# A transformer block on one core: order of a batch's attention pieces, cross-attention's query and key weights as one matrix per head, and both input norms from one variance

## The chip, the core and the metric

The kernel runs on one core of a Trainium2 chip. The core has a matrix engine (TensorE; PE in the profile, and PEld for its loads of the stationary operand), three engines for elementwise work (VectorE = DVE, ScalarE = ACT, GpSimd = POOL) and a queue that only issues transfers (SyncE = SP). Each engine works through its own list of instructions in order and waits on semaphores for the others. TensorE writes its results to PSUM, from which DVE or ACT copy them to SBUF. The metric is the device time of one execution in microseconds. The kernel before took 962.75 us, the median of three runs (961.74 to 963.99).

## The reference

The input x has 16 batches of 128 tokens of 128 features, all in float32. It goes through four residual parts; each part sees the layer norm of the stream. The change touches only the first part, which has a self-attention, a cross-attention with 77 context tokens per batch and a gated feed-forward part. Cut to what matters:

```python
def layernorm(x, eps=1e-05):
    m = jnp.mean(x, axis=-1, keepdims=True)
    v = jnp.var(x, axis=-1, keepdims=True)
    return (x - m) * jax.lax.rsqrt(v + eps)

def adaln(x, t, w, b):
    scale, shift = jnp.split(t @ w + b, 2, axis=-1)
    return layernorm(x) * (1.0 + scale) + shift

def mha(xq, ctx, wq, wk, wv, wo, bo):        # H = 16 heads of DH = 64
    q, k, v = heads(xq @ wq), heads(ctx @ wk), heads(ctx @ wv)
    scores = jnp.einsum('bhqd,bhkd->bhqk', q, k) / math.sqrt(DH)
    attn = jax.nn.softmax(scores, axis=-1)
    out = jnp.einsum('bhqk,bhkd->bhqd', attn, v)
    return out.transpose(0, 2, 1, 3).reshape(b, sq, INNER) @ wo + bo

# first part, called with layernorm(x) as x
h1 = adaln(x, t, norm1_w, norm1_b)
x = mha(h1, h1, attn1_wq, attn1_wk, attn1_wv, attn1_wo, attn1_bo) + x
h2 = adaln(x, t, norm2_w, norm2_b)
x = mha(h2, context, attn2_wq, attn2_wk, attn2_wv, attn2_wo, attn2_bo) + x
h3 = adaln(x, t, norm3_w, norm3_b)
x = glu_ff(h3, ff_w1, ff_b1, ff_w2, ff_b2) + x
```

So the input is normed twice in a row: the part is given layernorm(x), and its own adaln norms that again. The other three parts (a mixture of experts with two of seven, an attention of slots over the context, and a mixture with one of eight) are as they were.

## The kernel before

The residual stream r and the input x0 stay in SBUF, tokens on the partitions. The attention works in groups of two batches: groups 0 to 7 are the self-attention (ph = 0), 8 to 15 the cross-attention (ph = 1). One batch of a group is a unit, and a unit's 16 heads are handled in two halves of eight (hg = 0, 1).

- `attn_prologue` (L235) prepares a group. In self-attention it norms the input into r (`ln_stats`, L173, then `normalize`, L200), norms r once more into z, and adds the output bias to r (`row_add`, L227, on POOL). `ln_stats` takes the bn_stats of each half of the features, seven small DVE instructions, and the power -1/2 on POOL (L170). TensorE transposes z (`ta`, L224), and ACT scales and shifts it into hT (L251). Then come the queries and the keys (`pq`, L267): 8 matmuls of 256 columns for the queries and 8 of 256 (self) or 154 (cross: 2 x 77 tokens) for the keys, copied by ACT two at a time (L268), and the values (`pv`, L272, copied at L276).
- `scores` (L279) takes one half of a unit: eight matmuls (`s`, L286) with 64 rows each, in which an even and an odd head lie on the two halves of the array's rows; then the softmax: maximum and subtraction on DVE (L294, L296), exponential on ACT (L297), sum and reciprocal on DVE (L299, L300), and the multiplication with the reciprocal on POOL (L301).
- `attend_t` (L304) transposes the weights of a half in two tiles of four heads (`te`, L311); ACT copies the first tile, DVE the second (L312).
- `attend_v` (L315) multiplies with the values (`po`, L321); ACT copies the first half's result, DVE the second's (L325).
- `attn_project` (L327) makes the output projection of a unit (`ya`, L331), and DVE adds it to r (L335).

PSUM has two buffers for the scores, two for the transposes and two for all else (projections of a group, `po` and `ya` in turn). The main loop (L379) is one unit ahead with the scores and one unit behind with the projection:

```python
            if i == 0:
                if g + 1 < NG:
                    states[g + 1] = attn_prologue(g + 1, ap_)
            ...
                e_next = [scores(states[g1], i1, hg, ap_) for hg in range(2)]
            oT = ap_.tile([P, 8, P], F32, name=f"oT{g}_{i}", tag="oT")
            eT = [attend_t(states[g], i, hg, e[hg], ap_) for hg in range(2)]
            if late:
                attn_project(*late)
            for hg in range(2):
                attend_v(states[g], i, hg, eT[hg], oT)
```

This text gives priorities and not the final order: a scheduler in the language's tile framework lays each engine's instructions into one list before the run, and takes later work into gaps that it foresees. The list is fixed from then on. In it the norms of all eight self-attention groups stand early on DVE, ahead of and between the first scores.

All weights are loaded at the start on SP's queue: attention's four blocks of 1 MB (`wa`, L108, two of them first and two at 13.9 us), the rest behind. The host lays them out in `_layout`; for each attention there is a block with wq and wk side by side and one with wv and wo.

## Time and profile before

| what | value |
|---|---|
| median of three runs | 962.75 us |
| the profiled execution | 961.27 us |
| its span, first to last instruction | 959.5 us |
| mean granted TensorE clock | 0.939 |
| busy share PE, DVE, ACT, POOL | 87%, 67%, 43%, 39% |
| attention, last addition to r | 488.5 us |
| one group of self-attention | 30.8 us |
| one group of cross-attention | 27.4 us |

The page's first part gives each engine's busy time in the span, its second part the busy share in 40 equal slices as one digit each. In the lists of groups a line gives the source line, the engine, the operation, what it writes and reads with the shapes, how many, busy time and mean duration, and the idle time of the engine ahead of it with what ended it. A line of the timeline gives start, duration, engine, source line, operation and count, and in brackets the idle time before it and what ended that. A line of the windows gives the stretch, its length, and for each engine the busy time with its number of instructions. A float32 matmul stands in the trace as two instructions; its end is modelled, so starts are safer to read than durations.

### The profile page before, as it was taken

The numbers are of one execution on the slowest core, as the hardware profiler recorded it, in microseconds if no ns is written. First come the engines' busy times: TensorE is split into PE (matmuls) and PEld (weight loads), VectorE is DVE, ScalarE is ACT, GpSimd is POOL, SyncE is SP. The second block draws the span as 40 slices with busy tenths as digits, with TensorE's granted clock in tenths as the row PEclk, the third lists the DMA queues.
The fourth block names the chain that finished last, engine by engine and source line by source line (L and its number), as shares of the span: only waits on it lengthen the run. The fifth ranks groups of instructions, "written<-read, shape, count | busy, mean of one in ns | idle before, by whom it ended". The sixth has DMA issues, their size and how long they took to land.

```text
span 959.5 us, 16967 instructions
## 1 busy us (share of the span) xinstructions
PE 830.1 (87%) x6155; PEld 660.3 (69%) x6155; DVE 646.5 (67%) x1946; ACT 416.5 (43%) x873; POOL 369.9 (39%) x416
## 2 busy tenths in 40 slices
PE   5799999999999999999999978999746677775597
PEld 4477767677687777777866647999645556654586
DVE  4896668766775654555867794555687776768454
ACT  2445554455444444554342211444135767552132
POOL 2442323222322211233252206776254544443476
PEclk9899999999999999999999988999859998976699
DMA  8100000000000000000020015998300000012794
GB/s 325 40 2 1 1 1 2 1 1 1 1 2 1 1 1 2 1 1 1 2 71 12 23 61 166 320 331 271 99 1 1 1 1 1 1 31 58 253 341 149
DMA packets 29422, 61.87 MB, mean 64 GB/s; under 512 B 4250, under 2 KB 17901, under 8 KB 28699
## 3 DMA queue, kind: packets, MB, share of 16 engines
q1 hardware_dynamic: 25067, 51.70, 15.9%
q0 software_dynamic: 4272, 9.09, 3.1%
q8 instruction: 49, 0.80, 0.3%
q14 instruction: 34, 0.28, 0.1%
HBM read 54.01 MB, written 7.23 MB: 64 GB/s over the span
## 4 chain that ended last, share of the span: by engine, by line
PE 56%; DVE 21%; POOL 8%; DMA 7%; ACT 4%; issue 4%; SPq 0%; POOLq 0%; ACTq 0%; DVEq 0%
PE pq L267 11%; PE s L286 6%; PE po L321 5%; PE pv L272 5%; PE te L311 5%; PE ya L331 4%; DMA res<-ysm,tom 3%; PE gum L735 2%; PE h1n L979 2%; ACT eT L312 2%; DMA zsm<-tok,frmm 2%; PE su L898 2%; DMA zsn<-tok,frmn 2%; PE ynn L994 1%; POOL ym L170 1%
## 5 line engine op out<-in xcount | busy, mean ns | idle before, releaser
L301 POOL TENSOR_TENSOR e<-e,ri 128x1024 f32<-128x1024 f32 (+1 forms) x64 | 99.9, 1562 | 297.5 <-DVE ri L300 129.1
L294 DVE TENSOR_REDUCE mx<-s 128x8 f32<-128x1024 f32 (+1 forms) x64 | 64.3, 1006 | 95.7 <-PE s L286 95.7
L267 PE MATMUL pq<-ha,wa 128*128 128x256 f32 x384 | 97.3, 406 | 0.9 <-ACT ha L251 0.9
L286 PEld LDWEIGHTS s<-k,q 64*128 64x128 f32 x1024 | 69.9, 187 | 40.6 <-issue 40.5
L286 PE MATMUL s<-k,q 64*128 64x128 f32 (+1 forms) x1024 | 87.0, 287 | 8.1 <-DVE e L296 8.1
L311 PE MATMUL te<-ident,e 128*128 128x128 f32 (+1 forms) x512 | 75.7, 280 | 12.9 <-ACT eT L312 12.0
L267 PEld LDWEIGHTS pq<-ha,wa 128*128 128x128 f32 x384 | 70.6, 198 | 19.0 <-ACT q L268 3.6
L299 DVE TENSOR_REDUCE ri<-e 128x8 f32<-128x1024 f32 (+1 forms) x64 | 64.0, 1001 | 21.0 <-ACT e L297 20.8
L331 PE MATMUL ya<-wa,oT 128*128 128x128 f32 x512 | 72.4, 275 | 0.0
L311 PEld LDWEIGHTS te<-ident,e 128*128 128x128 f32 (+1 forms) x512 | 55.6, 144 | 23.7 <-ACT eT L312 8.5
L312 ACT COPY eT<-te 128x512 f32<-128x512 f32 (+1 forms) x64 | 37.3, 582 | 79.6 <-PE te L311 79.5
L321 PE MATMUL po<-eT,v 128*64 128x128 f32 (+1 forms) x1024 | 69.9, 278 | 0.0
L297 ACT ACTIVATE e<-e 128x1024 f32<-128x1024 f32 (+1 forms) x64 | 56.9, 891 | 29.5 <-DVE e L296 28.6
L296 DVE TENSOR_TENSOR e<-s,mx 128x1024 f32<-128x1024 f32 (+1 forms) x64 | 64.3, 1007 | 3.9 <-DVE mx L294 0.5
L331 PEld LDWEIGHTS ya<-wa,oT 128*128 128x128 f32 x512 | 64.4, 192 | 0.4 <-ACT oT L325 0.4
L321 PEld LDWEIGHTS po<-eT,v 128*64 128x64 f32 (+1 forms) x1024 | 56.4, 136 | 7.2 <-ACT oT L325 0.8
L735 PE MATMUL gum<-zTnm,wm 128*128 128x128 f32 x456 | 61.3, 275 | 0.0
L735 PEld LDWEIGHTS gum<-zTnm,wm 128*128 128x128 f32 x456 | 56.8, 192 | 0.3 <-ACT zTnm L650 0.2
L268 ACT COPY q<-pq 128x512 f32<-128x512 f32 x64 | 37.3, 584 | 45.3 <-PE pq L267 45.3
L636 POOL DMA_INDIRECT zsm<-tok,frmm x38 | 36.9, 970 | 34.1 <-DVE secm L614 21.1
L276 ACT COPY v<-pv 128x512 f32<-128x512 f32 (+1 forms) x64 | 37.4, 584 | 21.8 <-PE pv L272 21.1
L312 DVE COPY eT<-te 128x512 f32<-128x512 f32 (+1 forms) x64 | 42.7, 669 | 5.3 <-PE te L311 5.3
(368 smaller groups left out, 1805.6 us busy)
## 6 DMA issues: line engine op xcount, KB each, us to landing
wm<-in_moe_w_dram SPq DMA_DIRECT2D x38, 576.0 KB, 5.1
wn<-in_moe_w_dram SPq DMA_DIRECT2D x23, 578.0 KB, 5.5
wa<-in_attn_w_dram SPq DMA_DIRECT2D x4, 1024.0 KB, 7.5
ygm<-res SPq DMA_DIRECT2D x8, 256.0 KB, 3.8
tok<-stm SPq DMA_DIRECT2D x4, 258.0 KB, 3.3
tok<-stn SPq DMA_DIRECT2D x4, 258.0 KB, 3.2
x<-in_x_dram SPq DMA_DIRECT2D x8, 128.0 KB, 7.1
cb<-in_rows_dram SPq DMA_DIRECT2D x1, 1024.0 KB, 8.7
```

The costliest lines, as they stand in the source:

```text
L267: PE.matmul(pq[:, j, :n], lhsT=wqk[:, w : w + P], rhs=src, start=True, stop=True)
L286: PE.matmul(ps[:, par, j * nk : (j + 1) * nk], lhsT=st["qT"][h0 : h0 + DH, c, i * P : (i + 1) * P], rhs=st["kT"][h0 : h0 + DH, c, i * nk : ...
L294: V.tensor_reduce(mx, pv, AX.X, ALU.max)
L296: V.tensor_tensor(e, pv, mx.unsqueeze(3).to_broadcast([P, 2, 4, nk]), ALU.subtract)
L297: S.activation(e, e, AF.Exp, scale=1.0 / math.sqrt(DH))
L299: V.tensor_reduce(ri, e, AX.X, ALU.add)
L301: G.tensor_tensor(e, e, ri.unsqueeze(3).to_broadcast([P, 2, 4, nk]), ALU.mult)
L311: PE.transpose(t[:nk, j, :], e[:, par, j, :], ident)
L312: (S.copy if par == 0 else V.tensor_copy)(eT[:nk, par], t[:nk])
L321: PE.matmul(po[par * DH : (par + 1) * DH, j, :], lhsT=st["v"][:nk, i, 8 * hg + 2 * j + par, :], rhs=eT[:nk, par, j, :], start=True, stop=True,
L331: PE.matmul(y, lhsT=oT[:, c, :], rhs=st["wo"][:, 1024 + c * D : 1024 + (c + 1) * D], start=(c == 0), stop=(c == 7),)
L735: PE.matmul(ps[j][:, c * P : (c + 1) * P], lhsT=w[:, k : k + P], rhs=zT, start=True, stop=True)
```

## The change

Three things are changed, and all of them lie in the attention.

- Order: in a unit the next unit's first half of scores, this unit's first half of transposes and the late projection now come ahead of the second half of scores and transposes; the products with the values follow at the end.
- Cross-attention's scores: for each head wq and wk are multiplied into one 128x128 matrix (`fold`, once, in place of wq and wk in SBUF, in the first two units of group 4; the host lays the two transposed for that). The keys become, for each head, that matrix times the context (16 matmuls of 154 columns, copied three at a time), the queries are hT itself, and the scores of four heads are one matmul with 128 rows and 4 x 77 columns.
- Norms: in self-attention both norms of the input come from one variance v. The first is (v + eps)^(-1/2); the norm of the normed input has the factor ((1 + eps) v + eps^2)^(-1/2) on x minus its mean. One power on POOL gives both, and z and r are both made from x0.

```diff
--- before.py
+++ after.py
@@ -197,6 +197,21 @@
         V.tensor_scalar(mean, mean, 0.5, None, ALU.mult)
         return rs, mean
 
+    def variance(src, p, n, nm):
+        st = sm.tile([P, 4, 6], F32, name=f"st{nm}", tag="st")[:p, :n, :]
+        for i in range(n):
+            V.bn_stats(st[:, i, :], src[:, i, :])
+        me, qe, mo, qo = (st[:, :, k] for k in (1, 2, 4, 5))
+        dm, mean, q = (small(nm, k, p, n, "") for k in ("dm", "mv", "qq"))
+        V.tensor_tensor(dm, me, mo, ALU.subtract)
+        V.tensor_tensor(q, qe, qo, ALU.add)
+        V.scalar_tensor_tensor(dm, dm, 0.25, dm, ALU.mult, ALU.mult)
+        V.scalar_tensor_tensor(q, q, 1.0 / D, dm, ALU.mult, ALU.add)
+        V.tensor_tensor(mean, me, mo, ALU.add)
+        V.tensor_scalar(mean, mean, 0.5, None, ALU.mult)
+        return q, mean
     def normalize(dst, src, rs, mean, n):
         for i in range(n):
             V.tensor_scalar(
@@ -232,18 +247,33 @@
     GB = 2
     GT = GB * P
 
-    def attn_prologue(g, ap_):
+    def attn_norm(g):
         ph, gi = divmod(g, B // GB)
         b0 = gi * GB
         rg = r[:, b0 : b0 + GB, :]
         z = zp.tile([P, 4, D], F32, name=f"za{g}", tag="z")
         if ph == 0:
             xg = x0[:, b0 : b0 + GB, :]
-            rs, mean = ln_stats(xg, P, GB, f"i{g}")
+            v, mean = variance(xg, P, GB, f"i{g}")
+            q = small(f"j{g}", "qj", P, 4, "")
+            V.tensor_scalar(q[:, GB:], v, 1.0 + LN_EPS, LN_EPS * LN_EPS, ALU.mult, ALU.add)
+            V.tensor_scalar(q[:, :GB], v, LN_EPS, None, ALU.add)
+            rs = rsqrt(q, P, 2 * GB, f"j{g}", "")
+            normalize(z, xg, rs[:, GB:], mean, GB)
             normalize(rg, xg, rs, mean, GB)
-        rs, mean = ln_stats(rg, P, GB, f"j{g}")
-        normalize(z, rg, rs, mean, GB)
+        else:
+            rs, mean = ln_stats(rg, P, GB, f"j{g}")
+            normalize(z, rg, rs, mean, GB)
         row_add(rg, R_BO1 if ph == 0 else R_BO2, GB)
+        return z
+    def attn_prologue(g, ap_):
+        ph, gi = divmod(g, B // GB)
+        b0 = gi * GB
+        rg = r[:, b0 : b0 + GB, :]
+        z = attn_norm(g)
         t = transpose_n(z, P, GB, f"a{g}")
         hT = zp.tile([P, 512], F32, name=f"ha{g}", tag="h")
         for i in range(GB):
@@ -256,16 +286,28 @@
         nk = P if ph == 0 else NC
         kvT = hT if ph == 0 else ctxT[:, b0 * NC : (b0 + GB) * NC]
         wqk, wvo = w_att[2 * ph], w_att[2 * ph + 1]
-        qT = ap_.tile([P, 8, GT], F32, name=f"q{g}", tag="q")
-        kT = ap_.tile([P, 8, GT], F32, name=f"k{g}", tag="k")
         v = ap_.tile([P, GB, H, DH], F32, name=f"v{g}", tag="v")
-        for dst, src, w0, n in ((qT, hT, 0, GT), (kT, kvT, 1024, GB * nk)):
-            for c in range(0, 8, 2):
-                pq = psM.tile([P, 2, 256], F32, name=f"pq{g}_{w0}_{c}", tag="mm")
-                for j in range(2):
-                    w = w0 + (c + j) * P
-                    PE.matmul(pq[:, j, :n], lhsT=wqk[:, w : w + P], rhs=src, start=True, stop=True)
-                S.copy(dst[:, c : c + 2, :n], pq[:, :, :n])
+        if ph == 0:
+            qT = ap_.tile([P, 8, GT], F32, name=f"q{g}", tag="q")
+            kT = ap_.tile([P, 8, GT], F32, name=f"k{g}", tag="k")
+            for dst, src, w0, n in ((qT, hT, 0, GT), (kT, kvT, 1024, GB * nk)):
+                for c in range(0, 8, 2):
+                    pq = psM.tile([P, 2, 256], F32, name=f"pq{g}_{w0}_{c}", tag="mm")
+                    for j in range(2):
+                        w = w0 + (c + j) * P
+                        PE.matmul(pq[:, j, :n], lhsT=wqk[:, w : w + P], rhs=src, start=True, stop=True)
+                    S.copy(dst[:, c : c + 2, :n], pq[:, :, :n])
+        else:
+            qT = hT
+            kT = ap_.tile([P, H, GB * NC], F32, name=f"k{g}", tag="k")
+            for c in range(0, H, 3):
+                m = min(3, H - c)
+                pq = psM.tile([P, 3, GB * NC], F32, name=f"pk{g}_{c}", tag="mm")
+                for j in range(m):
+                    w = (c + j) * D
+                    PE.matmul(pq[:, j, :], lhsT=wqk[:, w : w + D], rhs=kvT, start=True, stop=True)
+                S.copy(kT[:, c : c + m, :], pq[:, :m, :])
         for i in range(GB):
             for hh in range(2):
                 pv = psM.tile([P, 8, DH], F32, name=f"pv{g}_{i}_{hh}", tag="mm")
@@ -276,11 +318,38 @@
                 S.copy(v[:nk, i, hh * 8 : (hh + 1) * 8, :], pv[:nk])
         return dict(ph=ph, b0=b0, nk=nk, qT=qT, kT=kT, v=v, wo=wvo, g=g)
 
+    def fold(w, hg):
+        ps = psS.tile([P, 2, 512], F32, name=f"fold{hg}", tag="s")
+        wp = w[:, hg * 1024 : (hg + 1) * 1024]
+        for j in range(4):
+            for par in range(2):
+                h0 = par * DH
+                PE.matmul(
+                    ps[:, par, j * D : (j + 1) * D],
+                    lhsT=wp[h0 : h0 + DH, (4 + j) * D : (5 + j) * D], rhs=wp[h0 : h0 + DH, j * D : (j + 1) * D],
+                    start=True, stop=True,
+                )
+        for par, copy in enumerate((S.copy, V.tensor_copy)):
+            copy(wp[:, par * 512 : (par + 1) * 512], ps[:, par, :])
     def scores(st, i, hg, ap_):
 
         nk, nm = st["nk"], f"{st['g']}_{i}_{hg}"
         ps = psS.tile([P, 2, 512], F32, name=f"s{nm}", tag="s")
-        for j in range(4):
+        if st["ph"] == 1:
+            for par in range(2):
+                h0 = 8 * hg + 4 * par
+                PE.matmul(
+                    ps[:, par, : 4 * nk].rearrange("p (j k) -> p j k", k=nk),
+                    lhsT=st["qT"][:, i * P : (i + 1) * P],
+                    rhs=st["kT"][:, h0 : h0 + 4, i * nk : (i + 1) * nk],
+                    start=True, stop=True,
+                )
+        for j in range(4 if st["ph"] == 0 else 0):
             for par in range(2):
                 h0, c = par * DH, 4 * hg + j
                 PE.matmul(
@@ -377,21 +446,30 @@
         late = None
         glu_h = {}
         for n, (g, i) in enumerate(units):
+            if n in (8, 9):
+                fold(w_att[2], n - 8)
             if i == 0:
                 if g + 1 < NG:
                     states[g + 1] = attn_prologue(g + 1, ap_)
                 else:
                     glu_h[0] = glu_prologue(0)
             e = e_next
-            if n + 1 < len(units):
+            more = n + 1 < len(units)
+            if more:
                 g1, i1 = units[n + 1]
-                e_next = [scores(states[g1], i1, hg, ap_) for hg in range(2)]
+                e_next = [None, None]
             oT = ap_.tile([P, 8, P], F32, name=f"oT{g}_{i}", tag="oT")
-            eT = [attend_t(states[g], i, hg, e[hg], ap_) for hg in range(2)]
+            eT = [None, None]
+            if more:
+                e_next[0] = scores(states[g1], i1, 0, ap_)
+            eT[0] = attend_t(states[g], i, 0, e[0], ap_)
             if late:
                 attn_project(*late)
-            for hg in range(2):
-                attend_v(states[g], i, hg, eT[hg], oT)
+            if more:
+                e_next[1] = scores(states[g1], i1, 1, ap_)
+            eT[1] = attend_t(states[g], i, 1, e[1], ap_)
+            attend_v(states[g], i, 0, eT[0], oT)
+            attend_v(states[g], i, 1, eT[1], oT)
             late = (states[g], i, oT)
         attn_project(*late)
 
@@ -1081,7 +1159,11 @@
     )[None]
     attn = []
     for k in ("attn1_", "attn2_"):
-        attn.append(cat([a[l0 + k + "wq"], a[l0 + k + "wk"]], axis=1))
+        if k == "attn1_":
+            attn.append(cat([a[l0 + k + "wq"], a[l0 + k + "wk"]], axis=1))
+        else:
+            q, kk = (chunks(a[l0 + k + w].T) for w in ("wq", "wk"))
+            attn.append(cat([q[:, :512], kk[:, :512], q[:, 512:], kk[:, 512:]], axis=1))
         attn.append(cat([a[l0 + k + "wv"], chunks(a[l0 + k + "wo"])], axis=1))
     f = "L0_ffn_"
     gs = [a[f + "sg"], *a[f + "rg"]]
```

## The prediction

> **What bounds the kernel now.** I read the page's busy shares and slices first, then the two attention stages by windows, then the TensorE and VectorE timelines inside them.
>
> ```profile
> PE 830.1 (87%) x6155; PEld 660.3 (69%) x6155; DVE 646.5 (67%) x1946; ACT 416.5 (43%) x873; POOL 369.9 (39%) x416
> ...
> PE   5799999999999999999999978999746677775597
> ...
> PEclk9899999999999999999999988999859998976699
> ```
>
> The attention fills slices 1 to 21 (its last addition to r ends at 488.5 us). There PE is at 9 and the clock full. Two windows, one group of two batches each, tell self- from cross-attention:
>
> ```profile
> 188.60:219.50 30.90, 29.14 (x236) 22.13 (x234) 22.67 (x35) 15.12 (x26) 9.08 (x7) 1.00 0.00 1
> 333.90:361.30 27.40, 27.09 (x237) 21.30 (x236) 16.09 (x35) 13.23 (x24) 6.69 (x7) 1.00 0.01 1
> ```
>
> A self-attention group takes 30.8 us (the scale and shift of h at L251 comes every 30.8 us), a cross-attention group 27.4 with PE idle for 0.3. So in cross-attention PE's own work sets the time, and what is taken from it comes off the end. What that work is:
>
> ```profile
> L286 PE MATMUL s<-k,q 64*128 64x77 f32 x512 | 41.5, 281 | 0.0
> ...
> 334.88 3.80 PE L267 MATMUL pq<-ha,wa 128*128 128x256 f32 x16
> 338.52 0.77 PE L267 MATMUL pq<-ctxT,wa 128*128 128x154 f32 x4
> ...
> 352.95 2.01 PE L286 MATMUL s<-k,q 64*128 64x77 f32 x30
> ```
>
> Each f32 matmul is two passes in the trace. From start to start a pass of 512 columns takes 0.429 us, of 256 0.216, of 154 0.131, of 128 0.112. A score pass, 64 rows, two side by side, takes 0.062 (2.01/30, less its tail) for 77 columns and the same for 128.
>
> In self-attention PE also stands still, for its VectorE neighbours:
>
> ```profile
> 215.88 0.66 PE L311 MATMUL te<-ident,e 128*128 128x128 f32 x4 [1.44 <-ACT eT L312]
> ...
> 213.03 1.23 DVE L296 TENSOR_TENSOR e<-s,mx 128x1024 f32<-128x1024 f32 x1
> 214.18 1.22 DVE L294 TENSOR_REDUCE mx<-s 128x8 f32<-128x1024 f32 x1
> 215.31 0.68 DVE L312 COPY eT<-te 128x512 f32<-128x512 f32 x1
> ```
>
> The copy that frees a transpose buffer stands on DVE behind the subtraction and the maximum of the next scores. And at the start:
>
> ```profile
> 35.35 0.77 PE L286 MATMUL s<-k,q 64*128 64x128 f32 x2 [5.97 <-DVE e L296]
> ...
> 32.67 1.21 DVE L294 TENSOR_REDUCE mx<-s 128x8 f32<-128x1024 f32 x1
> ```
>
> the first scores are ready at 29.0, but DVE is in the norms until 32.7, and PE waits 6 us.
>
> **1. Cross-attention: one matrix per head (8 groups).** Counting each pass to the start of the next, the window 333.9 to 361.3 divides into: queries 3.64, keys 2.62, scores 4.93, projection 4.40, attention times values 3.95, transposes 3.74, values 3.72, ta 0.37; sum 27.4.
> Removed: the queries' 16 passes, 3.64. Keys become 16 matmuls, 32 passes x 0.131 = 4.19, and about 0.5 of waiting where an exponential (0.72) gets between ACT's copies: 4.7, that is +2.1. Scores become two matmuls of 308 columns with 128 rows per unit and half: 16 passes x 0.259 (0.216 at 256 columns, plus 52 at the slope up to 512) = 4.14, that is -0.8. The projection is no longer cut by transposes in the built order: 32 x 0.112 = 3.6, -0.8; the values' products are cut twice more by scores, +0.2. Sum -2.9; walking the built PE order with these durations gives 24.4, and I take **-3.0 a group**. Ends: -3.6 (only the durations at full rate) and -1.6 (projection as slow as now, keys at the 0.164 of today's passes).
> ACT has fewer copies (six of up to 462 columns for eight; 512 take 0.58, 308 take 0.42) and isn't the bound. Does the softmax keep up? From scores to normalized weights: 0.80 + 0.80 + 0.72 + 0.79 + 0.19 + 1.23 (L294, L296, L297, L299, L300, L301) and five hand-overs of 0.1: 5.0 us. In the built order the second half's transposes in a unit without prologue come 8.0 us after their scores, so 3 us are left. One group's prologue falls into self-attention's last window, so I count 7.8 groups: 7.8 x -3.0 = **-23.4** (-28.1 to -12.5).
>
> The row that decides the scores is the packed pass: 0.062 at 77 columns and at 128, so it pays for something that doesn't shrink with the moving columns; the 128 stationary ones of its load (PEld L286, 187 ns each, two at a time) are the nearest. The Trainium skill, page "TensorEngine Tiling (Array Packing)", section "Theoretical Speedup", speaks against this edit: contractions of up to 64 rows run up to twice as fast packed, which the new scores give up. Taken at its word, an estimate from that page, a group would gain some 1.1 instead of 3.0 and the sum would be -14; the row disagrees with it at 77 columns.
>
> **2. The order of a batch's pieces (self-attention).** Per unit it was scores 0, scores 1, transposes 0 and 1, projection, products; now scores 0, transposes 0, projection, scores 1, transposes 1, products. No instruction is added. In the built order DVE's chain from one second-half score is: subtraction until 3.0 us after these scores, exponential, sum until 5.3, maximum of the next scores until 6.4, reciprocal, then GpSimd 1.9: the last transposes start at 8.9, where PE was free at 8.2 (wait 0.7, in place of today's 1.44 and its like). Behind it DVE does subtraction, sum, maximum, subtraction, copy, z (held by GpSimd's multiplication, as the 1.48 us z at 219.03 is today) and sum again, and frees the buffer of the next group's second query pair only at 15.9, where PE is ready at 14.1 (wait 1.8). Then the projections run, one exponential costing 0.3, and the group closes at 30.05: **-0.75** a group. Ends: today's excess in the projection (6.02 us against 32 x 0.112) goes altogether, -2.4; or a copy falls behind one more subtraction and maximum (2 x 1.13), +2.3. Five steady groups: **-3.8** (-12 to +11.5).
>
> **3. One variance for both norms.** Eight powers of 4 columns (1.04, L170) replace sixteen of 2 (0.70), and half the statistics go. First group: the chain at 8.84 to 11.84 (r, statistics, power, z) becomes z alone, so its projections start at 10.9 instead of 13.3. But the second group's x lands at 13.9 as before, and DVE's queue then holds, per group, a power of 1.04 and a row addition of 0.73 on POOL in turn with 1.2 of r or z: about 3.2 with z, 2.6 without, instead of 4.8. The first maximum comes at 29.9, not 32.7, the subtraction that frees PE 2.7 us earlier; and the seventh and eighth group's statistics, which today hold the third maximum until 51.6 where its scores are done at 49.9, are gone by then: 2.7 + 1.6, less a little: **-4** (0, if the loads set it, to -6). Later in self-attention these steps lie early on DVE and cost PE nothing either way.
>
> **4. The fold.** 16 matmuls of 64 rows, 32 passes x 0.062 = 2.0, and four copies of 128x512 (0.58 ACT, 0.67 DVE) in the fifth group. Its weights were issued at 14.3 and landed within 9.1, long before. The copies lie beside projections; without that cover the two on DVE cost 1.3. It takes one of two score buffers, which were free by then: **+2.1** (0 if it falls into the waits of part 2, to +3.4). No DMA is added, SP's order is the same list, and behind the attention every engine's order is unchanged.
>
> Sum: -23.4 - 3.8 - 4 + 2.1 = -29.1. The profiled execution took 961.3 (span 959.5, 1.8 around it): 932.2. The median of the runs is 962.75, 1.5 higher, and so I predict **934**. Its own range is 922 to 946. A difference of 0.2%, 1.9 us, is about what a measurement can tell from none.
>
> **The rivals.**
> *The softmax takes PE's place in cross-attention.* If DVE's queue delays the second half's weights by over 3 us, the group stays at 27.4 and only parts 2 to 4 are left: -5.7, 957. For it: DVE's line of sum, maximum, subtraction, copy, z. Against it: DVE is busy 16.1 of 27.4.
> *Packing is worth a full half.* 77 columns at the slope of 0.429 for 512 are 0.065 a pass, two side by side 0.032. If that is what the 64 passes cost and the rest of their 4.93 is waiting that the new passes inherit, scores cost 1.1 more instead of 0.8 less, a group gains 1.1: -8.6 - 5.7, 948. For it: nothing but the arithmetic; against it 30 passes in 2.01 us without a stop. This is what the tiling page's rule would give here.
> *The new scores' operand is slow.* Their moving side is four stretches of 77, 154 apart; no row has that form. Between the 0.259 of the slope, which I take because all f32 rows follow it, and twice that (16 x 0.259 = 4.1 more): a group loses 1.2, +9.4 - 5.7, 966.
> *Slower: the second half's copy on DVE.* The products of the second half now follow their transposes at once, and the copy that they need (L312, DVE) stands behind the next scores' maximum and subtraction. Where PE has nothing to put between, it waits 2 x 1.13 in each of 16 units, and 2 x 0.71 in the 16 of cross-attention: +59, with the rest 993. It decides from half of that, about 0.9 us a unit. For it: PE waits 1.44 for just such a copy today. Against it: in the built order ta, scores and query projections stand before seven of the eight products.
> *It doesn't do what it says.* The scheduler could undo the order; but in the built order the scores, transposes and projection do stand as in the edit, so I give it nothing of its own.
>
> Chances: forecast 0.74; softmax 0.11, 957; packing 0.04, 948; slow operand 0.04, 966; copies 0.07, 993. Faster is 0.74 + 0.11 + 0.04, with little lost at the forecast's edges: 0.89; slower 0.10, same 0.01. The range leaves out the two slower cases and the far ends, where all bounds of parts 1 to 3 would fall together, and takes in the softmax case: 919 to 958.
>
> **What would show it.** Right: cross-attention's group 24 to 25 us, PE still above 95% there; score passes of 308 columns near 0.26 apart; L286's 64-row form gone from cross-attention; self-attention's group near 30; the first long wait of PE ending near 32.7; the attention's last addition to r near 460. Wrong: PE waits of over 1 us at transposes or products in cross-attention, self-attention's group over 31, or a fold that holds the scores.

## The result, and the profile after

The changed kernel takes 934.26 us (median of four runs, 931.10 to 938.01) where the kernel before takes 962.25 (961.70 to 963.99): a ratio of 0.971 with a 95% interval of 0.967 to 0.975. The profiled execution took 934.72 us, with a span of 933.0.

All of it lies in the attention. On VectorE's timeline the last addition to r of the kernel before and that of the changed kernel (start, duration, engine, line, operation, then the idle time before it and what ended that):

```profile
488.17 0.29 DVE L335 TENSOR_TENSOR r<-ya,r 128x128 f32<-128x128 f32 x1 [1.28 <-PE ya L331]
```

```profile
460.86 0.29 DVE L404 TENSOR_TENSOR r<-ya,r 128x128 f32<-128x128 f32 x1 [1.28 <-PE ya L400]
```

The attention ends 27.3 us earlier; behind it come 471.0 us before and 471.8 after (span less the end of that addition). The page of the changed kernel, busy share and slices:

```profile
PE 814.3 (87%) x5803; PEld 645.8 (69%) x5803; DVE 633.9 (68%) x1900; ACT 408.8 (44%) x859; POOL 366.9 (39%) x408
...
PE   6799999999999999999999969999557777684697
...
PEclk9899999999999999999999989999669898976799
```

352 TensorE instructions are gone, and the attention is still a row of nines, at full clock from the third slice on. One group of self- and one of cross-attention, in windows (stretch, length, busy time and instructions of PE, PEld, DVE, ACT, POOL, then granted clock and the share and rate of transfers):

```profile
183.30:212.80 29.50, 28.66 (x236) 22.23 (x236) 21.71 (x36) 15.06 (x24) 9.02 (x6) 1.00 0.01 2
344.50:369.10 24.60, 24.60 (x188) 19.05 (x188) 15.56 (x29) 11.90 (x23) 5.62 (x5) 1.00 0.00 1
```

In the window of cross-attention PE has no idle time at all. Below, the attention is cut where ACT starts to scale and shift h for groups 3, 8, 9 and 15 (groups counted from 0; 8 is the first of cross-attention), and at the last addition to r. Lengths in us, and the difference to the kernel before:

| kernel | start to group 3 | five groups of self-attention, 3 to 8 | the turn, 8 to 9 | six groups of cross-attention, 9 to 15 | group 15 to the end | attention's end |
|---|---|---|---|---|---|---|
| before | 96.1 | 154.2 | 28.9 | 164.2 | 45.1 | 488.5 |
| changed | 92.4 (-3.7) | 149.5 (-4.7) | 28.7 (-0.2) | 147.8 (-16.4) | 42.7 (-2.4) | 461.2 (-27.3) |

The experiments are read by the same cuts, because these tell smaller differences than whole runs: the time behind the attention goes from 464.8 to 474.3 us among kernels whose work there is the same, while the changed kernel, profiled twice on two chips, gave attention ends of 461.15 and 461.20.

### The profile page after: what moved, and what is told of

Its sections match the earlier page's. It is cut to its first block, busy times and chain, and to the rows that moved or that the text cites. A ratio compares the mean times of both kernels' runs of the same rounds, so it can differ in the third digit from the quotient of the medians.

```text
span 933.0 us, 16193 instructions
## 1 busy us (share of the span) xinstructions
PE 814.3 (87%) x5803; PEld 645.8 (69%) x5803; DVE 633.9 (68%) x1900; ACT 408.8 (44%) x859; POOL 366.9 (39%) x408
## 3 DMA queue, kind: packets, MB, share of 16 engines
q1 hardware_dynamic: 25067, 51.70, 16.4%
## 4 chain that ended last, share of the span: by engine, by line
PE 56%; DVE 24%; POOL 8%; DMA 5%; issue 3%; ACT 3%; SPq 1%; POOLq 0%; ACTq 0%; DVEq 0%
PE pv L314 6%; PE po L390 5%; PE pq L298 5%; PE gum L813 5%; PE ya L400 4%; PE te L380 4%; PE pk L309 4%; PE s L346 4%; DVE mx L363 3%; PE ynm L824 2%; DVE e L365 2%; PE h1n L1057 2%; DVE ri L368 2%; DMA zsn<-tok,frmn 2%; PE su L976 2%
## 5 line engine op out<-in xcount | busy, mean ns | idle before, releaser
L380 PE MATMUL te<-ident,e 128*128 128x128 f32 (+1 forms) x512 | 71.7, 276 | 4.8 <-POOL e L370 4.7
L390 PE MATMUL po<-eT,v 128*64 128x128 f32 (+1 forms) x1024 | 75.3, 279 | 0.5 <-DVE eT L381 0.3
L390 PEld LDWEIGHTS po<-eT,v 128*64 128x64 f32 (+1 forms) x1024 | 60.7, 137 | 15.5 <-DVE eT L381 8.6
L298 PE MATMUL pq<-ha,wa 128*128 128x256 f32 x256 | 66.4, 410 | 1.4 <-ACT ha L281 0.9
L400 PE MATMUL ya<-wa,oT 128*128 128x128 f32 x512 | 63.1, 276 | 0.0
L400 PEld LDWEIGHTS ya<-wa,oT 128*128 128x128 f32 x512 | 59.9, 192 | 1.1 <-ACT v L318 0.6
L298 PEld LDWEIGHTS pq<-ha,wa 128*128 128x128 f32 x256 | 47.7, 201 | 14.3 <-ACT q L299 2.4
L355 PE MATMUL s<-k,q 64*128 64x128 f32 x512 | 44.0, 290 | 7.4 <-DVE e L365 7.4
L355 PEld LDWEIGHTS s<-k,q 64*128 64x128 f32 x512 | 34.8, 188 | 17.8 <-issue 14.9
L735 POOL DMA_INDIRECT res<-ysm,tom x38 | 37.3, 982 | 16.4 <-ACT ysm L828 6.2
```

The costliest lines, as they stand in the source:

```text
L298: PE.matmul(pq[:, j, :n], lhsT=wqk[:, w : w + P], rhs=src, start=True, stop=True)
L355: PE.matmul(ps[:, par, j * nk : (j + 1) * nk], lhsT=st["qT"][h0 : h0 + DH, c, i * P : (i + 1) * P], rhs=st["kT"][h0 : h0 + DH, c, i * nk : ...
L380: PE.transpose(t[:nk, j, :], e[:, par, j, :], ident)
L390: PE.matmul(po[par * DH : (par + 1) * DH, j, :], lhsT=st["v"][:nk, i, 8 * hg + 2 * j + par, :], rhs=eT[:nk, par, j, :], start=True, stop=True,
L400: PE.matmul(y, lhsT=oT[:, c, :], rhs=st["wo"][:, 1024 + c * D : 1024 + (c + 1) * D], start=(c == 0), stop=(c == 7),)
```

## The experiments

**Each part alone, and the matrices without the shared load.** Four kernels on one chip, where the kernel before took 962.93 us (median of 29 runs). The first makes only the new order:

```diff
-                e_next = [scores(states[g1], i1, hg, ap_) for hg in range(2)]
...
-            eT = [attend_t(states[g], i, hg, e[hg], ap_) for hg in range(2)]
...
+                e_next[0] = scores(states[g1], i1, 0, ap_)
+            eT[0] = attend_t(states[g], i, 0, e[0], ap_)
             if late:
                 attn_project(*late)
-            for hg in range(2):
-                attend_v(states[g], i, hg, eT[hg], oT)
...
+                e_next[1] = scores(states[g1], i1, 1, ap_)
+            eT[1] = attend_t(states[g], i, 1, e[1], ap_)
+            attend_v(states[g], i, 0, eT[0], oT)
+            attend_v(states[g], i, 1, eT[1], oT)
```

> The kernel before with the new order of a unit's pieces alone. By the prediction's terms the order takes 3.8 us from self-attention and, in cross-attention, 0.8 a group from the projection that is no longer cut, less 0.2 for the products that are cut more often: 3.8 + 0.6 x 7.8 = 8.5, so 954. Rival 1, the matrix per head carries nearly all of the gain: 960 to 962. Rival 2, the order carries it and the matrix per head little: 940 to 945.

The second takes only cross-attention's matrices with the fold, in the old order and with two norms:

```diff
+            if n in (8, 9):
+                fold(w_att[2], n - 8)
...
-        for dst, src, w0, n in ((qT, hT, 0, GT), (kT, kvT, 1024, GB * nk)):
...
+        else:
+            qT = hT
+            kT = ap_.tile([P, H, GB * NC], F32, name=f"k{g}", tag="k")
...
```

> The kernel before with cross-attention's one matrix per head alone, in the old order. By the prediction's terms a group loses 3.64 of queries and 0.8 of scores and gains 2.1 of keys, 2.35 x 7.8 = 18.3, less 2.1 for the multiplication of the weights: 16, so 946. Rival 1: 936 to 938. Rival 2: 955 or more.

The third takes only the one variance:

```diff
-            rs, mean = ln_stats(xg, P, GB, f"i{g}")
+            v, mean = variance(xg, P, GB, f"i{g}")
...
+            rs = rsqrt(q, P, 2 * GB, f"j{g}", "")
+            normalize(z, xg, rs[:, GB:], mean, GB)
             normalize(rg, xg, rs, mean, GB)
-        rs, mean = ln_stats(rg, P, GB, f"j{g}")
-        normalize(z, rg, rs, mean, GB)
...
```

> The kernel before with one variance for both norms alone. By the prediction -4, so 958, with the first long wait of the matrix engine ending near 33.5 as in the changed kernel. Rival: the seconds gained at the start are lost again in the next groups, which wait for the softmax and not for the norms: 961 to 963.

The fourth is the changed kernel, with the scores of cross-attention head by head, so that hT is loaded anew for each 77 columns:

```diff
-                PE.matmul(
-                    ps[:, par, : 4 * nk].rearrange("p (j k) -> p j k", k=nk),
-                    lhsT=st["qT"][:, i * P : (i + 1) * P],
-                    rhs=st["kT"][:, h0 : h0 + 4, i * nk : (i + 1) * nk],
...
+                for j in range(4):
+                    PE.matmul(
+                        ps[:, par, j * nk : (j + 1) * nk],
+                        lhsT=st["qT"][:, i * P : (i + 1) * P],
+                        rhs=st["kT"][:, 8 * hg + 4 * par + j, i * nk : (i + 1) * nk],
...
```

> The changed kernel with each cross-attention head's scores as a matmul of its own: 128 rows and 77 columns, eight per half, instead of two of 308. The moving columns are the same in sum. If a short pass is paid by the load of its 128 stationary columns, a pass takes 0.112 as in the projection: 64 x 0.112 = 7.2 us a group for 4.6, +2.6 x 8 = +20, so 954 or a little more. If the moving columns alone counted, 77 columns would take 0.065 and the time would stay at 934.

| kernel | median, us | ratio to before (95%) | start to 3 | 3 to 8 | turn | 9 to 15 | 15 to end | attention's end |
|---|---|---|---|---|---|---|---|---|
| order alone | 955.11 | 0.994 (0.992 to 0.996) | -0.1 | -8.8 | -0.3 | +1.4 | +1.8 | 482.5 (-5.9) |
| matrices alone | 946.51 | 0.983 (0.979 to 0.986) | +0.8 | +3.8 | -1.6 | -15.1 | 0.0 | 476.3 (-12.1) |
| one variance alone | 957.82 | 0.995 (0.993 to 0.998) | -3.5 | +0.3 | 0.0 | +0.3 | 0.0 | 485.5 (-3.0) |
| all, scores by head | 954.43 | 0.992 (0.989 to 0.995) | -3.8 | -4.7 | +0.5 | -0.4 | +1.8 | 482.0 (-6.5) |

The totals came out within 1.2 us of the expectations, but the stretches say more. The order alone met its total of 954 by two misses: self-attention gained 8.8 us where 3.8 was expected, and cross-attention lost 3.2 where a gain of 4.7 was. The three parts alone sum to -21.0 at the attention's end, together they give -27.3. In self-attention and at the start they nearly add up (-8.8 + 3.8 + 0.3 = -4.7, and -2.8 against -3.7). Behind the turn they do not: order and matrices alone give +1.4 - 15.1 + 0.3 = -13.4 in the six groups and +1.8 at the end, together they give -16.4 and -2.4, that is 7.1 us more than the sum; the turn gives 1.7 back. So the new order costs 3.2 us in cross-attention with the old queries, keys and packed scores, and it gains there with the new ones. What PE spends from the start of each pass to the start of the next (worked out from the trace, us for one group of cross-attention; a wait counts with the piece ahead of it):

| | before | order alone | matrices alone | changed | by head |
|---|---|---|---|---|---|
| queries | 3.64 | 3.64 | none | none | none |
| keys | 2.62 | 2.62 | 4.52 | 4.51 | 4.57 |
| scores | 4.94 | 4.87 to 5.77 | 4.50 | 4.60 | 7.01 |
| projection | 4.40 | 3.76 | 4.40 | 3.57 | 3.57 |
| products with values | 3.95 | 4.35 to 4.67 | 4.10 | 4.50 | 4.73 |
| transposes | 3.74 | 3.87 to 3.93 | 3.67 | 3.73 | 3.69 |

(Columns of the order alone: two groups, 28.3 and 27.0 us long. Windows by head hold some passes of the neighbouring group.)

The order takes the interruptions out of the projection (-0.6 to -0.8, of which 0.3 are two waits of 0.16 for ACT's copies) and lengthens the products (+0.4 to +0.7). The 5.77 of the scores with the order alone holds a wait. In every second of these groups PE stands still for VectorE's copy of the second half's transposes, which the new order puts just ahead of the products that need it. PE's timeline of the order alone:

```profile
344.75 1.09 PE L321 MATMUL po<-eT,v 77*64 77x128 f32 x14 [0.66 <-DVE eT L312]
```

Three such waits make 2.0 of the 3.2 us, and the changed kernel has none of them in cross-attention. So the rival that the prediction calls the copies came true in part, in the kernel with the order alone. The other 1.2 us were not taken apart. A part of them is likely that PE goes more often to or from a piece that uses only half of the array's rows (packed scores, 64*128 in the lines) or half of its columns (products, 77*64): 15 times in a group before, 16 and 19 with the order alone, and 8 with the new matrices in either order, at about 0.1 us each (the next section has the lines for that).

By head, the whole gain of the matrices is gone: the group is back at 27.3. PE's groups of one cross-attention group, by form, in that kernel and in the changed one (count, then busy time and mean duration, whose ends are modelled):

```profile
L346 PE MATMUL s<-k,ha 128*128 128x77 f32 x64 | 8.4, 273 | 0.0
```

```profile
L346 PE MATMUL s<-k,ha 128*128 128x308 f32 x16 | 5.4, 437 | 0.0
```

and their starts on PE's timelines, by head first, then the changed kernel:

```profile
366.08 1.91 PE L346 MATMUL s<-k,ha 128*128 128x77 f32 x16
367.83 1.04 PE L380 MATMUL te<-ident,e 128*77 128x128 f32 x8
```

```profile
356.58 1.21 PE L346 MATMUL s<-k,ha 128*128 128x308 f32 x4
357.63 1.03 PE L380 MATMUL te<-ident,e 128*77 128x128 f32 x8
```

Sixteen passes of 77 columns take 1.75 us to the start of the next work, 0.109 each; four of 308 take 1.05, 0.262 each. Both do the same scores. A pass of 77 columns is not shorter than one of 128 (0.112 in the projection), a pass of 308 stands on the slope of the long ones (0.216 for 256, 0.429 for 512). The 128 columns of the stationary side are the same in the first two, and four heads under one load cost 0.066 a head where four loads cost 0.109. That it is the stationary side that sets the short pass, and not a least time of any pass, is seen in two small pieces behind the attention, on PE's timeline of the changed kernel at full clock:

```profile
485.58 1.04 PE L535 MATMUL plm<-gatew,zTm 128*128 128x7 f32 x8
486.47 2.82 PE L509 MATMUL glu<-hg,gluw 128*128 128x512 f32 x6
```

```profile
661.05 0.65 PE L877 MATMUL plc<-wl,hc 128*77 128x1 f32 x8
```

Passes with 128 stationary and only 7 moving columns are 0.111 apart (0.89 for eight); those with 77 stationary columns and one moving column are 0.069 apart in a steady run. The Trainium skill, page "TensorE: Matmul & The Clock Gate", section "LDWEIGHTS (loading the stationary operand)", has the time of a load go with its columns and not its rows, 107 ns for 128 as an estimate from its formula. The spacing of the short passes, 0.109 to 0.112, agrees with it; the records of these loads last longer, 192 ns in the mean of the kernel by head, and overlap.

**The order in self-attention only; where the fold and one copy stand.** The rest ran on two other chips, on which the kernel before takes 1004.69 and 1005.92 us; their totals compare only as ratios, or within one chip, while the attention's end compares with the table above (the last section shows where the difference lies). In the first of these kernels the groups of cross-attention keep the old order:

```diff
+            if g < NG // 2:
                 ...new order...
+            else:
...
+                if n + 1 < len(units):
...
+                    e_next = [scores(states[g1], i1, hg, ap_) for hg in range(2)]
...
+                eT = [attend_t(states[g], i, hg, e[hg], ap_) for hg in range(2)]
+                if late:
+                    attn_project(*late)
+                for hg in range(2):
+                    attend_v(states[g], i, hg, eT[hg], oT)
```

> The changed kernel with the new order in self-attention alone, and the old order in cross-attention. The prediction gave the new order 0.6 us a group in cross-attention (0.8 from the projection, less 0.2): without it 24.63 would become 25.2 and the time 934 + 4.7 = 939. The traces of the two parts alone say less: 24.85 a group with the matrix per head in the old order, so +0.2 x 7 = 1.5 at most at the attention's end, 934 to 936, which this measurement can hardly tell from 934; the group's length in the trace decides.

The second moves the fold to the start, ahead of the first scores:

```diff
         states = {0: attn_prologue(0, ap_)}
+        for hg in range(2):
+            fold(w_att[2], hg)
...
-            if n in (8, 9):
-                fold(w_att[2], n - 8)
...
-        for par, copy in enumerate((S.copy, V.tensor_copy)):
+        for par, copy in enumerate((S.copy, S.copy)):
```

> The changed kernel with the fold ahead of the first scores, all its copies on the scalar engine. The fold's group takes 31.7 us where its neighbours take 29.5, and at the start the matrix engine waits 6.6 us for the vector engine. If the fold hides in that wait, 2.2 us go, and the second group's first query pairs, which now stand ahead of the waiting scores, take 1.7 more out of it: attention's end near 457, 930. Rival: the later scores hold up the first softmax by the fold's 2 us and nothing is gained: 934.

The third has ACT make both copies of a second half's transposes in self-attention:

```diff
-            (S.copy if par == 0 else V.tensor_copy)(eT[:nk, par], t[:nk])
+            (S.copy if par == 0 or (hg == 1 and st["ph"] == 0) else V.tensor_copy)(eT[:nk, par], t[:nk])
```

> The changed kernel with both copies of the second half's transposes on the scalar engine in self-attention. If the vector engine's queue is what sets the matrix engine's wait at the last transposes (0.70 a group), it goes, with some of what stands behind it: -0.7 to -1.4 a group in eight groups, 929 to 923. Rival: self-attention is set by the matrix engine's own passes and switches, and the scalar engine, which then has 1.2 us more a group, delays exponentials instead: 934 or more.

| kernel | median, us | ratio to before (95%) | start to 3 | 3 to 8 | turn | 9 to 15 | 15 to end | attention's end |
|---|---|---|---|---|---|---|---|---|
| order in self-attention only | 978.78 | 0.973 (0.968 to 0.978) | -3.9 | -4.7 | -0.2 | -15.2 | 0.0 | 464.5 (-24.0) |
| fold at the start | 976.25 | 0.971 (0.968 to 0.974) | -0.9 | -8.8 | -0.2 | -16.3 | -2.4 | 459.9 (-28.5) |
| copies on ACT | 976.24 | 0.971 (0.968 to 0.974) | -1.6 | -4.0 | -3.3 | -16.8 | -2.4 | 460.4 (-28.1) |

With the new matrices, the new order in cross-attention is worth 1.1 us in six groups and 2.4 behind them. Taking the fold out of group 4 is worth 4.1 us in self-attention, twice what its passes take; the start gives 2.8 of them back: the built list then holds eleven more instructions of norms ahead of VectorE's first maximum, which comes at 34.53 instead of 30.78. With the copies on ACT the turn is 3.1 us shorter, but the start is 2.1 longer and self-attention 0.7; the attention ends 0.8 us earlier, and the total does not tell the kernel from the changed one. The 5 to 11 us that were expected if VectorE's copies set the wait of 0.70 did not come; the profile puts that wait down to POOL's multiplication (the lines are in the next section).

**Fold in the wait, copy at the turn, and the changed kernel again.** At the start PE has a wait of 6.56 us, for a score buffer that the first subtraction frees:

```profile
26.55 0.44 PE L239 MATMUL ta<-ident,za 128*128 128x128 f32 x2
33.55 0.76 PE L355 MATMUL s<-k,q 64*128 64x128 f32 x2 [6.56 <-DVE e L365]
```

One kernel lets the fold use two buffers of the projections instead of a score buffer, and puts it behind the first scores:

```diff
-        ps = psS.tile([P, 2, 512], F32, name=f"fold{hg}", tag="s")
+        ps = [psM.tile([P, 512], F32, name=f"fold{hg}_{par}", tag="mm") for par in range(2)]
...
-        for par, copy in enumerate((S.copy, V.tensor_copy)):
-            copy(wp[:, par * 512 : (par + 1) * 512], ps[:, par, :])
+        for par in range(2):
+            S.copy(wp[:, par * 512 : (par + 1) * 512], ps[par])
...
         e_next = [scores(states[0], 0, hg, ap_) for hg in range(2)]
+        for hg in range(2):
+            fold(w_att[2], hg)
...
-            if n in (8, 9):
-                fold(w_att[2], n - 8)
```

> The fold stands behind the first two scores, in two PSUM tiles of the pool of the projections instead of one score tile, with all its copies on ACT; its 32 passes stand on TensorE where it waits 6.6 us for the first subtraction. If the fold's 2.2 us in the fifth group are TensorE's own time and the start has the room, that group goes back to 29.5 us, the start takes at most 1 us more (half of the passes stand behind the wait), and the attention ends 1 to 2 us before the changed kernel's 461.2: about 459.7. If the start loses as it did in the kernel with the fold ahead of the first scores (the first maximum at 34.5 instead of 30.8), it ends at 461 to 463. In the total either is within 0.2% of the changed kernel, 0.970 of the time before.

Another gives ACT the second copies of the last self-attention group alone:

```diff
-            (S.copy if par == 0 else V.tensor_copy)(eT[:nk, par], t[:nk])
+            (S.copy if par == 0 or (hg == 1 and st["g"] == NG // 2 - 1) else V.tensor_copy)(eT[:nk, par], t[:nk])
```

> One group's copies of second-half transposes (the last of self-attention) go to ACT instead of VectorE. If those copies, behind VectorE's maximum and subtraction, are what holds the products where self-attention turns into cross-attention, the interval there falls from 28.7 to about 25.6 us, as it did with all of self-attention's second copies on ACT, and nothing else moves: the attention ends at 458.1 instead of 461.2, the total 0.967 of the time before. If that interval had only handed time on to its neighbours, the end stays at 461.

A third makes both edits:

> Both of these edits together. If they are independent, the attention ends at about 456.6 and the total is 0.965 to 0.966 of the time before; if one gives back what the other gains, 459 to 461.

And the changed kernel ran beside them:

> The changed kernel once more, beside the three others on the same chip: 0.971 of the time before, the attention's last addition to r at 461.2, and whatever differs between chips lies behind that.

| kernel | median, us | ratio to before (95%) | start to 3 | 3 to 8 | turn | 9 to 15 | 15 to end | attention's end |
|---|---|---|---|---|---|---|---|---|
| fold in the wait | 971.70 | 0.966 (0.963 to 0.969) | -2.5 | -8.8 | -0.2 | -16.3 | -2.4 | 458.4 (-30.1) |
| copy at the turn | 974.16 | 0.969 (0.966 to 0.971) | -2.7 | -4.7 | -1.3 | -16.8 | -2.4 | 460.6 (-27.9) |
| both | 971.88 | 0.967 (0.963 to 0.970) | -2.0 | -8.8 | -1.3 | -16.8 | -2.4 | 457.2 (-31.3) |
| the changed kernel again | 978.68 | 0.973 (0.971 to 0.976) | -3.7 | -4.7 | -0.2 | -16.3 | -2.4 | 461.2 (-27.3) |

The fold in the wait does what was expected and a little more: all of self-attention's groups take 29.1 us, the start loses 1.3, and the attention ends 2.8 us earlier. Its interval lies below that of the changed kernel on the same chip. The 7 us between the medians are more than the attention explains; the rest of the difference lies behind it, in the stretch that varies anyway. PE's timeline at the start of that kernel shows half of the fold just ahead of the wait, which still ends at 33.61 (33.55 in the changed kernel), and the other half behind it, where it costs time. The wait is not shorter, because in this run the first scores came 1.3 us earlier:

```profile
25.16 1.06 PE L331 MATMUL fold<-wa 64*128 64x128 f32 x16
26.15 0.44 PE L239 MATMUL ta<-ident,za 128*128 128x128 f32 x2
33.61 1.19 PE L355 MATMUL s<-k,q 64*128 64x128 f32 x6 [7.01 <-DVE e L365]
35.08 1.28 PE L331 MATMUL fold<-wa 64*128 64x128 f32 x6 [0.28 <-ACT wa L337]
```

The copy at the turn missed: 1.1 us at the turn and 0.5 in the next groups instead of 3.1, and the start is 1.0 longer, so that the end moves by 0.6. With all second copies on ACT one group of self-attention had grown from 29.5 to 30.7, so a part of the 3.1 had only changed places. Both edits together end the attention earliest, 4.0 us before the changed kernel, but the total doesn't tell them from the fold alone.

## Why the prediction was right, point by point

The forecast was 934, the median 934.26; the profiled execution was put at 932.2 and took 934.7. The end of the attention was put 29.1 us earlier and came 27.3 earlier. That closeness is luck in good part: three of the four terms were off, with opposite signs, and the order of the pieces by more than a factor of two.

**Cross-attention: the mechanism right, the term too large (-23.4 put, -18.9 measured).** A full group lost 2.73 us where 3.0 was put; six of them are 16.4. The rest, for which 1.8 further groups had been counted, that is 5.4, measured 0.2 at the turn and 2.4 at the end. Within a group, the queries (-3.64), the keys (+1.9 for +2.1) and the projection (-0.83 for -0.8) are as put. Three items are not. The scores gained 0.34 instead of 0.8: in a run of four the passes take 0.262, near the 0.259 that was put, but a pass just ahead of products or behind them takes 0.35 to 0.37, so the mean is 0.287. The products lost 0.55 instead of 0.2; the kernels with the order alone (+0.4 to +0.7) and the matrices alone (+0.15) show that this is mostly the order's doing. And the values (-0.24) and the transposes of z (-0.09) gained what was put at nothing. The first two are no waits:

```profile
358.60 1.31 PE L390 MATMUL po<-eT,v 77*64 77x128 f32 x18
359.83 0.53 PE L346 MATMUL s<-k,ha 128*128 128x308 f32 x1
```

Eighteen products, 0.062 each in a steady run, take 1.23 us to the next start where 1.12 would be the rate: the change leaves about 0.1. Not every change does: in the lines of the kernel by head and the changed kernel above, passes of 77 and of 308 columns go over to transposes at their steady rate (0.109 and 0.262). There both sides use all rows of the array and more than half of its columns (128*128 and 128*77 in the lines); products use half of its columns (77*64), and packed scores half of its rows (64*128). The values gained in the same way: in the traces their last pass ahead of packed scores takes 0.52 us and ahead of transposes 0.43.

**The order of the pieces: the wait that was to come next didn't (-3.8 put, -8.8 measured).** The kernels with the order alone and with the fold in the wait both show groups of 29.1, 1.76 us shorter than before, where 0.75 was put. The first wait of the prediction came to the hundredth, in all five groups of each of these two kernels. PE's timeline of the order alone, one line of each of two neighbouring groups:

```profile
122.43 1.09 PE L311 MATMUL te<-ident,e 128*128 128x128 f32 x8 [0.70 <-POOL e L301]
151.51 1.09 PE L311 MATMUL te<-ident,e 128*128 128x128 f32 x8 [0.70 <-POOL e L301]
```

The second one, 1.8 us of the next group's second query pair for a buffer that VectorE's oT copy frees, is the step that failed. PE's and VectorE's timelines of the changed kernel:

```profile
186.22 0.49 PE L390 MATMUL po<-eT,v 128*64 128x128 f32 x4
186.64 1.13 PE L298 MATMUL pq<-ha,wa 128*128 128x256 f32 x4
```

```profile
187.83 0.68 DVE L394 COPY oT<-po 128x512 f32<-128x512 f32 x1
```

The four passes of that pair start at 186.64, 1.2 us before the copy starts, and without a wait. By the semaphores in the trace the second pair waits for ACT alone, whose copy of the first pair (185.31 to 185.89) empties its buffer; it is the third pair that waits for VectorE, and the oT copy is through (188.51) when its turn comes (188.56). The walk had put the wait one pair too early: the two buffers do not change hands strictly in turn. Without those 1.8 us the walk would have closed at 28.25; 29.1 came, so some 0.8 us were missing in it, and the runs don't say at which pieces. Against the kernel before, a group's waits fell from 1.76 to 0.74 us, the projection without its waits from 4.25 to 3.76, the scores from 5.17 to 4.92 and the values from 3.70 to 3.60; the transposes rose from 3.72 to 3.85.

The prediction also misread the wait of 1.44 that the order was to remove. It gave it to VectorE's copy, but its line names ACT's. ACT's timeline of the kernel before:

```profile
214.29 1.06 ACT L297 ACTIVATE e<-e 128x1024 f32<-128x1024 f32 x1 [1.74 <-DVE e L296]
215.26 0.57 ACT L312 COPY eT<-te 128x512 f32<-128x512 f32 x1
```

ACT's copy stood behind an exponential, which had waited for VectorE's subtraction; it ended at 215.83, and the transposes started at 215.88, before VectorE's copy was through (215.99). The wait went all the same, but it was no case of the wait that the rival of the copies describes.

**One variance: right (-4 put, -3.7 together and -3.5 alone).** The first maximum, on VectorE's timeline of the changed kernel:

```profile
30.78 1.22 DVE L363 TENSOR_REDUCE mx<-s 128x8 f32<-128x1024 f32 x1
31.92 0.34 DVE L217 TENSOR_SCALAR r<-x,mvi,yj 128x128 f32<-128x128 f32 x1
32.19 1.22 DVE L365 TENSOR_TENSOR e<-s,mx 128x1024 f32<-128x1024 f32 x1
```

It comes at 30.78 instead of 32.67, where 29.9 was put, and PE goes on at 33.55 instead of 35.35, 1.8 us earlier and not 2.7; the rest of the gain is made by group 3. Nothing of it shows later: one variance alone changes the other stretches by 0.3 at most.

**The fold: undersized, beyond its bound (+2.1 put, up to +3.4; +4.1 measured).** Its passes took about what was put, 1.1 to 1.2 us for each half; but it stands on PE's path in full and holds a score buffer, so that the next scores wait for the subtraction ahead of them. PE's timeline of the changed kernel:

```profile
172.18 1.16 PE L331 MATMUL fold<-wa 64*128 64x128 f32 x16
174.04 0.46 PE L355 MATMUL s<-k,q 64*128 64x128 f32 x2 [0.69 <-DVE e L365]
```

The prediction had named a fold that holds the scores as a thing that would prove it wrong, and took the score buffers to be free. The waits themselves are small: 0.17 in one half, and in the other the 0.69 stands in place of the 0.70 at the transposes. All of PE's waits in the five groups sum to 4.25 us, against 3.68 with the fold in the start's wait. Passes and waits make 2.8 of the 4.1 us. The groups before and behind the fold's two are longer as well (29.44 and 29.54 instead of 29.08), and in the second of them the built list cuts scores and transposes once more each; what makes up the whole of the last 1.3 us was not settled.

Together: cross-attention 4.5 short, the order 5.0 over, the fold 2.0 short, the variance 0.3 short; -29.1 + 4.5 - 5.0 + 2.0 + 0.3 = -27.3, as measured.

**The rivals.** The softmax did not take PE's place: PE is busy in 24.60 of 24.60 us. The slow operand did not come: four stretches of 77 columns run at 0.262 a pass, on the slope. The copies of the second half on VectorE hardly held the products of the changed kernel, whose waits in the whole attention sum to 0.5 us, 0.3 of them for these copies (with the order alone they held them for 2.0 us in cross-attention); on the page of the changed kernel:

```profile
L390 PE MATMUL po<-eT,v 128*64 128x128 f32 (+1 forms) x1024 | 75.3, 279 | 0.5 <-DVE eT L381 0.3
```

On packing the prediction was right in its number and wrong in its argument. It said that the row disagrees with the rule of the Trainium skill, page "TensorEngine Tiling (Array Packing)", section "Theoretical Speedup", of up to twice the speed. The kernel by head shows that the rule holds: without packing, a head's pass costs 0.109 where a packed one took 0.062, 1.8 times, and the edit would have gained nothing. What made it harmless to give packing up is not that packing is worth nothing at 77 columns, but that one load serves four heads.

## What to carry to other kernels

A short matmul is paid by its stationary load, as long as its moving columns are fewer than the stationary ones: when packed passes are to be given up for full ones, see that many moving columns share one load, or the gain is lost (0.109 us a head against 0.066 and a packed 0.062). When two edits meet in one list, read them stretch by stretch: an order of pieces that cost 3.2 us in cross-attention with the old matrices, 2.0 of them in waits for one copy, gained 3.5 with the new ones, and no sum of single parts shows that. One-off work belongs in a wait that is there, in buffers for which nothing else is queued: the fold cost 4.1 us in a full group and 1.3 in the start's wait.

## What the runs showed of the hardware that was not expected

On the two other chips the kernel before takes 4.3 and 4.5% longer. In the changed kernel none of that is in the attention (461.2 both times). The page's row of transfer rates in 40 slices, first the changed kernel on the first chip, then the same kernel on another:

```profile
GB/s 323 53 1 1 1 2 1 1 1 2 1 1 1 1 2 1 2 1 1 48 27 24 48 153 207 333 309 170 76 0 1 1 1 2 12 23 58 265 343 155
```

```profile
GB/s 328 31 1 1 2 1 1 1 2 1 1 2 1 1 2 1 1 1 14 57 23 28 165 108 235 233 235 163 73 1 1 1 2 1 12 65 188 215 217 120
```

The loads at the start run at the same 323 and 328 GB/s; the streams of expert weights, which follow behind the attention and are not among the loads at the start, reach 333 and 343 on one chip and stay at 235 and 217 on the other, and the stretch behind the attention grows from 471.8 to 514.9 us. The slower rate and the longer stretch go together; that the one makes all of the other was not tried, nor whether it is the chip or other traffic at the time that lowers the rate.
